# A three-stage latent transformer kernel: the first latent group's opening dealt out anew over the engines, four key products side by side, and identity products on TensorE while it waits

## The chip, the cores and the metric

The kernel runs on one core of one Trainium2 chip. The metric is device time in microseconds (us), the median over several executions. The engines are named as in the profile: PE (TensorE matmul), PEld (its weight load), DVE (VectorE), ACT (ScalarE), POOL (GpSimd) and SP (SyncE, which issues most of the DMAs).

## The reference, cut to what matters

`x` has shape (16, 64, 512), the context (16, 512, 512). Three residual blocks follow one another; the change is in the first steps of the first block.

```python
x = x + _L0_xattn_ref(ctx_1024, _layernorm(x), mask, g_x, b_x, g_l, b_l, w_q, w_kv, w_out, g_o, b_o)
x = x + _L0_attn_ref(_layernorm(x), Wq, Wk, Wv, Wo, ...)
x = x + _L0_ffn_ref(_layernorm(x), w_gate, w_up, w_down)

def _L0_xattn_ref(x, latents, mask, g_x, b_x, g_l, b_l, w_q, w_kv, w_out, g_o, b_o):
    xn = _ln(x, g_x, b_x)                        # the context
    ln = _ln(latents, g_l, b_l)                  # the 64 latents of each batch
    q = ln @ w_q
    kv_in = jnp.concatenate([xn, ln], axis=1)
    k, v = jnp.split(kv_in @ w_kv, 2, axis=-1)
    ...                                          # 8 heads of 64, softmax over 512 + 64 keys
    return _ln(out @ w_out, g_o, b_o)
```

## The kernel before, in words

The 16 x 64 latent rows are eight tiles `x0` to `x7` of 128 rows by 512. `_latents` makes q, k and v of the latents (products named `lq`, `lk`, `lv`), two tiles at a time: four groups of two tiles. Then `cross_attention` runs over the 16 batches, and after it come self-attention and the feed-forward block. All weights and activations of the large products are split into a high part (rounded to fp32r) and a low part (the remainder), so that a product is three terms: high x high, low x high, high x low, each over four chunks `k` of 128 of the contraction (`Common.terms`, the matmuls of L121).

A group of latents is made by these helpers of `_latents`:

- `moments(p)` (L494 to L500): bn_stats and bn_aggr of tile `p` on DVE, then two one-column instructions on POOL that make the reciprocal root.
- `norm(p)`: one DVE instruction over 128x512 into `lz`.
- `turn(p)` (L506): four PE transposes of `lz` into PSUM `lt` (L171), then four instructions of 128x128 that apply gain and offset into `ln`, on ACT (L520), or on DVE for tile 1 (L518).
- `upper(p)` and `lower(p)`: DVE makes the high part `lnh` (L526) and the low part `lnl` (L532).
- `high(name, w, k)` (L479): ACT rounds chunk `k` of a weight into its high part. `low(name, w, k)` (L483): DVE or POOL subtracts it for the low part. The raw weights `raw_k`, `raw_q`, `raw_v` (four chunks of 256 KB each) come by DMA into nine buffers, so that the last three chunks of `raw_v` wait for a chunk of `raw_k` to be done with.
- `bias("q", k)` (L538, L541): DVE adds up the raw query weight's chunks, weighted by `b_x`, into `ws_bq`; `bias_sum` sums that over the partitions on PE (`bq`, L549) and takes it out on DVE (L556).
- `CrossWeights.load` and `turn`: four small DMAs of the vectors g_l, b_l, b_x, g_x into `vec_rows`, one PE transpose (`vec_t`), one ACT copy (`vec`), and b_l - b_x on POOL.

`heads(g, what, ...)` makes the products `lk` or `lq` of group `g`: four column blocks of 128, each of 12 matmuls with 256 columns, taken out by ACT into `kst` (L600) or `qst` (L602). For the keys of group 0 `late = 3`: the first three blocks run together, term by term, and the fourth after them. `values(g)` makes `lv`, 24 matmuls with 512 columns. PSUM has three buffers for `mm`/`tr` tiles, two for `two` (tag "sim"), one for `av`.

The order of instructions on each engine is the order of the program text, with work that is spread over the products in between: `during(n, f)` puts `f` behind the n-th column block (`then()` is called after each). The opening, ahead of the first product, is written out at the end of `_latents`: loads, `moments(0)`, `cw.turn()`, `norm(0)`, and so on. Engines take their instructions in order; an instruction that waits holds up those behind it on its engine.

Of the kernel before, what the change touches and what calls it, by code (L numbers as in the profile page):

```python
# [9 lines left out]
F32 = mybir.dt.float32  # L10
# [4 lines left out]
ALU = mybir.AluOpType  # L15
# [4 lines left out]
P = 128  # L20
D = 512
KC = D // P
# [11 lines left out]
LN_EPS = 1e-5  # L34
# [11 lines left out]
def f32(t):  # L46

    return t.bitcast(F32)


class Common:
# [62 lines left out]
    def terms(self, ps, parts, ks, start=True, stop=True):  # L114

        terms = [(0, 2), (0, 3), (1, 2)]
        n, last = 0, len(terms) * len(ks) - 1
        for i, j in terms:
            for k in ks:
                p = parts(k)  # L120
                self.nc.tensor.matmul(  # L121
                    ps, lhsT=p[i], rhs=p[j], start=start and n == 0, stop=stop and n == last
                )
                n += 1
            yield

    def split(self, hi, lo, src, by=None):

# [86 lines left out]
GT = GB // 2  # L215
# [80 lines left out]
class Context:  # L296
# [74 lines left out]
class CrossWeights:  # L371
# [13 lines left out]
    def load(self, pool):  # L385
        self.rows = pool.tile([len(self.NAMES) * KC, P], F32, tag="vec", name="vec_rows")
        for n, name in enumerate(self.NAMES):
            self.cm.nc.sync.dma_start(
                self.rows[n * KC : (n + 1) * KC, :], self.i[name].rearrange("(c p) -> c p", p=P)
            )  # L390

    def turn(self):
        cm, nc = self.cm, self.cm.nc
        n = len(self.NAMES) * KC
        pt = cm.tr("vec_t")[:, :n]
        nc.tensor.transpose(pt, self.rows, cm.ident[:n, :n])
        nc.scalar.copy(self.vec, pt)

        nc.gpsimd.tensor_tensor(self.bl, self.bl, self.bx, ALU.subtract)


class SelfConstants:
# [52 lines left out]
def _latents(ctx, tc, cm, sc, i, cw, cx, sa):  # L455
    nc = tc.nc
# [12 lines left out]
    def load(*tiles):  # L469
        for p in tiles:  # L470
            nc.sync.dma_start(cm.x[p], i["x"][p * P : (p + 1) * P, :])
# [3 lines left out]
            raws[name, k] = pool.tile([P, D], F32, tag="raw", bufs=9, name=f"raw_{name}_{k}")  # L475
            nc.sync.dma_start(raws[name, k], source[name][k * P : (k + 1) * P, :])

    def high(name, w, k):
        nc.scalar.copy(w[0][:, k, :], raws[name, k])  # L479

    def low(name, w, k, by=None):
        by = by or (nc.vector, nc.gpsimd)[k % 2]
        by.tensor_tensor(w[1][:, k, :], raws[name, k], f32(w[0][:, k, :]), ALU.subtract)  # L483
# [6 lines left out]

    def moments(p):
        st = cm.small.tile([P, 6], F32, tag="st", name=f"st_l_{p}")  # L494
        mv = mvs[p] = cm.small.tile([P, 2], F32, tag="mv", name=f"mv_l_{p}")
        nc.vector.bn_stats(st, cm.x[p])
        nc.vector.bn_aggr(mv, st)
        r = mv[:, 1:2]
        nc.gpsimd.tensor_scalar(r, r, 1.0 + LN_EPS, LN_EPS * LN_EPS, ALU.mult, ALU.add)
        nc.gpsimd.tensor_tensor(r, r, cm.mhalf[:, :1], ALU.pow)  # L500
# [5 lines left out]
    def turn(p):  # L506
# [7 lines left out]
        ln = pool.tile([P, KC, P], F32, tag="ln", bufs=2, name=f"ln_{p}")  # L514
        for k in range(KC):
            src, scale, bias = pt[:, k * P : (k + 1) * P], cw.gl[:, k : k + 1], cw.bl[:, k : k + 1]
            if p == 1:
                nc.vector.tensor_scalar(ln[:, k, :], src, scale, bias, ALU.mult, ALU.add)  # L518
            else:
                nc.scalar.activation(ln[:, k, :], src, AF.Identity, bias=bias, scale=scale)  # L520
        rows[p] = ln

    def upper(*tiles):
        for p in tiles:
            g, n = divmod(p, GT)
            nc.vector.tensor_copy(lns[g][0][:, :, n * P : (n + 1) * P], rows[p])  # L526

    def lower(*tiles):
        for p in tiles:
            g, n = divmod(p, GT)  # L530
            hi, lo = (t[:, :, n * P : (n + 1) * P] for t in lns[g])
            nc.vector.tensor_tensor(lo, rows.pop(p), f32(hi), ALU.subtract)  # L532

    def bias(name, k):

# [45 lines left out]
    def during(n, do, *args):  # L581

        todo.setdefault(n, []).append((do, args))
# [9 lines left out]
    def heads(g, what, w, dst, scale, bias=None):  # L593

        hi, lo = lns[g]
        st = pool.tile([P, KC, GT * P], F32, tag=f"{what}st", name=f"{what}st_{g}")

        def take(m, ps):
            if bias is None:
                nc.scalar.copy(st[:, m, :], ps)  # L600
            else:
                nc.scalar.activation(  # L602
                    st[:, m, :], ps, AF.Identity, bias=bias[:, m : m + 1], scale=scale
                )


        late = 3 if (g, what) == (0, "k") else 0
        lag = 2 if (g, what) == (0, "q") else 0
        made, ready = [], []
        for m in range(KC):  # L610
            cols = slice(m * P, (m + 1) * P)
            ps = cm.mm(f"l{what}_{g}_{m}")[:, : GT * P]
            terms = cm.terms(
                ps,
                lambda k, cols=cols: (w[0][:, k, cols], w[1][:, k, cols], hi[:, k, :], lo[:, k, :]),
                range(KC),
            )
# [12 lines left out]
        for at, done, _ in ready:  # L630
            take(at, done)
        nc.sync.dma_start(dst[g], st)

    def values(g):
        hi, lo = lns[g]
        for n, p in enumerate(groups[g]):
# [1068 lines left out]
```

## Time and profile before

| | us |
|---|---|
| median of 5 runs | 918.62 (918.1 to 919.25) |
| the profiled execution's own time | 918.1 |
| its span, first to last instruction | 916.3 |
| PE busy in the span | 896.1 |
| DVE / ACT / POOL busy | 688.8 / 392.8 / 328.9 |
| first matmul of `lk` (group 0) | 11.67 |
| first matmul of `lv` (group 0) | 28.25 |

Times in the profile count from the start of the span. 1.8 us of the profiled execution's time lie outside the span. The columns of the stage rows are: stretch, its length, then busy time and number of instructions for PE, PEld, DVE, ACT and POOL, the granted clock, the DMA engines' share and GB/s. A timeline row gives start, length, engine, line, operation, out<-in, shape, count, and in brackets the idle time before and what ended it.

### The profile page before, as it was taken

To read this page: it belongs to the slowest core of one execution; us is meant where nothing else is said; L and a number is where in the kernel's file an instruction comes from. 1 tells how busy PE (TensorE), PEld (TensorE's weight loads), DVE (VectorE), ACT (ScalarE), POOL (GpSimd) and SP (SyncE) were. 2 spreads that over 40 slices of the span, in tenths; PEclk is the share of its full clock that TensorE was granted. 3 is DMA by queue.
4 is the path that set the end of the run, shared out by engine and by line. 5 is a ranking of instruction groups with operands and counts; after the bars stand their busy time and mean duration, and the time that the engine had idled before them with its cause. 6 is when DMAs were issued, how large, how long until landed. Compare 5 with 4: busy or idle time off the path is not lost.

```text
span 916.3 us, 17531 instructions
## 1 busy us (share of the span) xinstructions
PE 896.1 (98%) x6774; PEld 741.0 (81%) x6774; DVE 688.8 (75%) x1386; ACT 392.8 (43%) x750; POOL 328.9 (36%) x376
## 2 busy tenths in 40 slices
PE   5999999999999999999999999999999999999998
PEld 5898777878787788787878887878778788888886
DVE  7544477788799787786987864576887698888875
ACT  4464444444454444444544455434444333322221
POOL 5245153335253353252533522565564320100000
PEclk9999999999999999999999999999999999999999
DMA  7564565554564445444644351140005530000000
GB/s 237 177 242 138 161 185 158 170 162 143 150 187 153 140 146 165 129 132 139 201 134 147 105 169 70 48 184 3 1 1 232 206 138 12 13 12 12 13 12 23
DMA packets 80234, 111.11 MB, mean 121 GB/s; under 512 B 33160, under 2 KB 38808, under 8 KB 78872
## 3 DMA queue, kind: packets, MB, share of 16 engines
q1 hardware_dynamic: 79992, 109.48, 36.6%
q8 instruction: 53, 0.87, 0.4%
q0 software_dynamic: 160, 0.52, 0.2%
q14 instruction: 29, 0.24, 0.1%
HBM read 84.26 MB, written 25.72 MB: 120 GB/s over the span
## 4 chain that ended last, share of the span: by engine, by line
PE 88%; DVE 7%; ACT 2%; issue 1%; POOL 1%; DMA 0%; DVEq 0%; ACTq 0%; POOLq 0%
PE pv L121 19%; PE pk L121 19%; PE gu L121 13%; PE dn L121 7%; PE av L904 4%; PE sim L836 4%; PE prt L171 3%; PE lv L121 2%; PE po L121 2%; PE lq L121 2%; PE lk L121 2%; PE wo L121 2%; PE Wv L121 2%; PE ht L171 1%; PE Wq L121 1%; PE Wk L121 1%
## 5 line engine op out<-in xcount | busy, mean ns | idle before, releaser
L121 PE MATMUL pv<-xvh,x 128*128 128x512 f32 x512 | 133.1, 392 | 0.0
L121 PE MATMUL pk<-x,xkh 128*128 128x512 f32 x512 | 130.5, 397 | 0.0
L121 PEld LDWEIGHTS pk<-x,xkh 128*128 128x128 f32 x512 | 93.7, 188 | 25.5 <-issue 3.9
L121 PEld LDWEIGHTS pv<-xvh,x 128*128 128x128 f32 x512 | 95.3, 188 | 23.3 <-issue 2.2
L810 DVE TENSOR_TENSOR k<-pk,row 128x512 f32<-128x512 f32 x64 | 43.7, 684 | 46.3 <-PE pk L121 46.2
L823 ACT ACTIVATE v<-pv,rs 128x512 f32<-128x512 f32 x64 | 43.9, 686 | 79.3 <-PE pv L121 79.2
L859 ACT ACTIVATE pr<-pr,least 128x576 f32<-128x576 f32 x64 | 49.2, 772 | 55.4 <-DVE least L855 55.1
L368 POOL TENSOR_TENSOR x<-raw,x 128x512 fp32r<-128x512 f32 x32 | 43.7, 1365 | 78.0 <-ACT x L362 71.8
L121 PE MATMUL pk<-x,xkl 128*128 128x512 f32 x256 | 68.7, 390 | 0.0
L121 PE MATMUL pv<-xvl,x 128*128 128x512 f32 x256 | 68.5, 389 | 0.0
L121 PE MATMUL gu<-uT,fx 128*128 128x512 f32 (+1 forms) x288 | 67.3, 377 | 0.0
L121 PE MATMUL gu<-gT,fx 128*128 128x512 f32 (+1 forms) x288 | 65.5, 375 | 1.1 <-DVE h L1541 0.6
L121 PEld LDWEIGHTS gu<-gT,fx 128*128 128x128 f32 x288 | 52.2, 188 | 9.0 <-ACT fx L129 0.9
L121 PEld LDWEIGHTS gu<-uT,fx 128*128 128x128 f32 x288 | 51.9, 188 | 7.2
L121 PEld LDWEIGHTS pk<-x,xkl 128*128 128x128 f32 x256 | 48.1, 188 | 10.4
L121 PEld LDWEIGHTS pv<-xvl,x 128*128 128x128 f32 x256 | 48.1, 188 | 10.2
L855 DVE CUSTOM_DVE_ANT_0 pr<-sim,mask 128x576 f32<-128x576 f32 x64 | 45.9, 755 | 6.3 <-PE sim L836 5.6
L121 PE MATMUL dn<-dT,hh 128*128 128x512 f32 x176 | 44.8, 394 | 0.6 <-ACT hh L129 0.6
L321 DVE BATCH_NORM_STATS2 cst<-nat 128x6 f32<-128x512 f32 x64 | 42.8, 669 | 3.4 <-DMA nat<-in_ctx_dram 3.4
L205 ACT ACTIVATE qe_h<-qe_h,mmagic 128x512 f32<-128x512 f32 (+1 forms) x24 | 16.5, 688 | 67.2 <-DVE qe_h L202 64.1
L871 ACT COPY prT<-prt 128x512 f32<-128x512 f32 x64 | 34.1, 585 | 18.1 <-PE prt L171 18.1
L904 PEld LDWEIGHTS av<-v,prT 128*64 128x64 f32 x1024 | 36.7, 138 | 5.6 <-issue 5.6
(302 smaller groups left out, 1976.5 us busy)
## 6 DMA issues: line engine op xcount, KB each, us to landing
nat<-in_ctx_dram SPq DMA_DIRECT2D x16, 1024.0 KB
raw<-in_ctxT_dram SPq DMA_DIRECT2D x64, 256.0 KB
d_d<-qhl_d SPq DMA_DIRECT2D x11, 512.0 KB
row<-rs_d SPq DMA_DIRECT2D x16, 256.0 KB
g_d<-qhl_g SPq DMA_DIRECT2D x8, 512.0 KB
u_d<-qhl_u SPq DMA_DIRECT2D x8, 512.0 KB
gT<-g_d SPq DMA_DIRECT2D x4, 1024.0 KB
uT<-u_d SPq DMA_DIRECT2D x4, 1024.0 KB
```

The lines of the kernel that those rows point to most:

```text
L121: self.nc.tensor.matmul(ps, lhsT=p[i], rhs=p[j], start=start and n == 0, stop=stop and n == last)
L171: self.nc.tensor.transpose(pt[:, c * P : (c + 1) * P], src[:, c * P : (c + 1) * P], self.ident)
L205: nc.scalar.activation(e, e, AF.Relu, bias=self.mmagic, scale=MAGIC)
L321: nc.vector.bn_stats(st, self.nat[b][:, j, :])
L368: by.tensor_tensor(lo, self.raw[:, c, :], f32(hi), ALU.subtract)
L810: nc.vector.tensor_tensor(k[:, S : S + N], ps, cx.row[b], ALU.mult)
L823: nc.scalar.mul(v, ps, cx.rs[b][:, t : t + 1])
L836: nc.tensor.matmul(pss[r][c * S : (c + 1) * S, h, :half], lhsT=queries[b % 2][rows, m, :], rhs=st["k"][m][rows, at : at + half], start=Tru ...
L855: nc.vector.tensor_tensor_reduce(two(pr), ps[:, :, :half], two(mask), -1.0, BIG, ALU.add, ALU.min, least)
L859: nc.scalar.activation(pr, pr, AF.Exp, bias=least, scale=-1.0, accum_out=st["tot"][:, t : t + 1])
L871: nc.scalar.copy(prT, pt.rearrange("p (j q) -> p j q", q=P))
L904: nc.tensor.matmul(st["av"][rows, 2 * a + r, :], lhsT=w[:, rows], rhs=v[:, at : at + S], start=(n == 0), stop=(n == len(pairs) - 1),)
```

## The change

The change is in the opening and in the order of some work behind it:

- The four `vec_rows` DMAs are issued by ACT, ahead of its table load, in place of SP.
- For tiles 0 and 1 the first of the two one-column instructions runs on DVE; `stats(1)` runs before `norm(0)`. b_l - b_x moves behind both roots on POOL.
- Key weights: chunks 0 and 1 are rounded on ACT ahead of `turn(0)`, chunk 2 on DVE ahead of `norm(1)`, chunk 3 on ACT behind tile 1's share.
- Tile 1's gain and offset: chunks 0 and 1 on ACT, 2 and 3 on DVE (all four on DVE before). `upper(0)` comes before, `upper(1)` behind it.
- `late = KC`: all four key blocks of group 0 run side by side, one matmul of each in turn, since `terms` now yields after each matmul; the fourth block lies in the `av` buffer of PSUM. All other products keep their order.
- All four low parts of the query weight are made on DVE (two of them on POOL before).
- Value weights: the high parts of chunks 0 to 3 are called behind blocks 3 to 6 and the low parts behind 4, 4, 7, 7 (1 to 4 and 2 to 5 before).
- `busy(n)`: n matmuls of the 128x128 identity with itself into a PSUM tile `idle` that nothing reads: 4 before `vec_t`, 6 behind it, 2 behind the transposes of tile 0, 4 behind those of tile 1.

In the built program the engines' orders differ from before in this opening alone, but for one ACT instruction far behind: `fz` of tile 2 (L166, at 700.06 us) stands two instructions later.

```diff
@@ Common.terms
                 n += 1
-            yield
+                yield
@@ CrossWeights
-            self.cm.nc.sync.dma_start(
+            self.cm.nc.scalar.dma_start(
...
-        nc.gpsimd.tensor_tensor(self.bl, self.bl, self.bx, ALU.subtract)
+    def less(self):
+
+        self.cm.nc.gpsimd.tensor_tensor(self.bl, self.bl, self.bx, ALU.subtract)
@@ _latents
-    def high(name, w, k):
-        nc.scalar.copy(w[0][:, k, :], raws[name, k])
+    def high(name, w, k, vector=False):
+        copy = nc.vector.tensor_copy if vector else nc.scalar.copy
+        copy(w[0][:, k, :], raws[name, k])
...
+    def stats(p):
+        mvs[p, "st"] = cm.small.tile([P, 6], F32, tag="st", name=f"st_l_{p}")
+        nc.vector.bn_stats(mvs[p, "st"], cm.x[p])
...
-        nc.gpsimd.tensor_scalar(r, r, 1.0 + LN_EPS, LN_EPS * LN_EPS, ALU.mult, ALU.add)
+        by = nc.vector if p < GT else nc.gpsimd
+        by.tensor_scalar(r, r, 1.0 + LN_EPS, LN_EPS * LN_EPS, ALU.mult, ALU.add)
...
-        late = 3 if (g, what) == (0, "k") else 0
+        late = KC if (g, what) == (0, "k") else 0
...
-            ps = cm.mm(f"l{what}_{g}_{m}")[:, : GT * P]
+            name = f"l{what}_{g}_{m}"
+            ps = cm.ps_av.tile([P, D], F32, tag="av", name=name) if m == late - 1 else cm.mm(name)
+            ps = ps[:, : GT * P]
...
-            for _ in range(3):
-                for _, _, steps in made:
-                    next(steps)
+            for _ in range(3 if late else 1):
+                for _ in range(KC if late else 3 * KC):
+                    for _, _, steps in made:
+                        next(steps)
...
+    idle = cm.two("idle")[:, 0, :P]
+
+    def busy(n):
+
+        for _ in range(n):
+            nc.tensor.matmul(idle, lhsT=cm.ident, rhs=cm.ident, start=True, stop=True)
+
+    cw.load(pool)
     load(0, 1)
-    cw.load(pool)
...
+    busy(4)
+    cw.turn()
+    stats(0)
     moments(0)
-    cw.turn()
+    stats(1)
     norm(0)
     moments(1)
+    cw.less()
+    high("k", w_k, 0)
+    high("k", w_k, 1)
+    busy(6)
+    turn(0)
+    high("k", w_k, 2, True)
     norm(1)
-    high("k", w_k, 0)
-    turn(0)
-    turn(1)
-    for k in range(1, KC):
-        high("k", w_k, k)
-    upper(0, 1)
+    busy(2)
+    turn(1, range(2))
+    busy(4)
+    upper(0)
+    weighed(1, range(2, KC), True)
+    upper(1)
+    high("k", w_k, 3)
     lower(0, 1)
...
     for k in range(KC):
-        low("q", w_q, k)
+        low("q", w_q, k, nc.vector)
...
-        during(1 + k, high, "v", w_v, k)
-        during(2 + k, low, "v", w_v, k)
+        during(3 + k, high, "v", w_v, k)
+        during((4, 4, 7, 7)[k], low, "v", w_v, k)
```

More of the change, by code (lines that the diff above doesn't have):

```diff
@@ L488, in split @@
             low(name, w, k)
+    def stats(p):
+        mvs[p, "st"] = cm.small.tile([P, 6], F32, tag="st", name=f"st_l_{p}")
+        nc.vector.bn_stats(mvs[p, "st"], cm.x[p])
     def moments(p):
-        st = cm.small.tile([P, 6], F32, tag="st", name=f"st_l_{p}")
+        if (p, "st") not in mvs:
+            stats(p)
         mv = mvs[p] = cm.small.tile([P, 2], F32, tag="mv", name=f"mv_l_{p}")
-        nc.vector.bn_stats(st, cm.x[p])
-        nc.vector.bn_aggr(mv, st)
+        nc.vector.bn_aggr(mv, mvs.pop((p, "st")))
         r = mv[:, 1:2]
-        nc.gpsimd.tensor_scalar(r, r, 1.0 + LN_EPS, LN_EPS * LN_EPS, ALU.mult, ALU.add)
+        by = nc.vector if p < GT else nc.gpsimd
+        by.tensor_scalar(r, r, 1.0 + LN_EPS, LN_EPS * LN_EPS, ALU.mult, ALU.add)
         nc.gpsimd.tensor_tensor(r, r, cm.mhalf[:, :1], ALU.pow)
@@ L504, in norm, with turn @@
         cm.normalize(zs[p], cm.x[p], f"l_{p}", mvs.pop(p))
-    def turn(p):
+    def turn(p, ks=range(KC)):
         g, n = divmod(p, GT)
@@ L513, in turn, with weighed @@
         cm.transpose_chunks(pt, zs.pop(p), KC)
-        ln = pool.tile([P, KC, P], F32, tag="ln", bufs=2, name=f"ln_{p}")
-        for k in range(KC):
+        rows[p] = pt, pool.tile([P, KC, P], F32, tag="ln", bufs=2, name=f"ln_{p}")
+        weighed(p, ks)
+    def weighed(p, ks, vector=False):
+        pt, ln = rows[p]
+        for k in ks:
             src, scale, bias = pt[:, k * P : (k + 1) * P], cw.gl[:, k : k + 1], cw.bl[:, k : k + 1]
-            if p == 1:
+            if vector:
                 nc.vector.tensor_scalar(ln[:, k, :], src, scale, bias, ALU.mult, ALU.add)
@@ L520, in turn @@
                 nc.scalar.activation(ln[:, k, :], src, AF.Identity, bias=bias, scale=scale)
-        rows[p] = ln
     def upper(*tiles):
@@ L525, in upper @@
             g, n = divmod(p, GT)
-            nc.vector.tensor_copy(lns[g][0][:, :, n * P : (n + 1) * P], rows[p])
+            nc.vector.tensor_copy(lns[g][0][:, :, n * P : (n + 1) * P], rows[p][1])
     def lower(*tiles):
@@ L531, in lower @@
             hi, lo = (t[:, :, n * P : (n + 1) * P] for t in lns[g])
-            nc.vector.tensor_tensor(lo, rows.pop(p), f32(hi), ALU.subtract)
+            nc.vector.tensor_tensor(lo, rows.pop(p)[1], f32(hi), ALU.subtract)
     def bias(name, k):
```

## The prediction

> **What bounds the kernel now.** I read the stages first: busy time in stretches of 10 us.
>
> ```profile
> core 0: us, PE busy (x) PEld busy (x) DVE busy (x) ACT busy (x) POOL busy (x), PEclk, DMA share, GB/s
> 0.00:10.00 10.00, 2.48 (x9) 1.61 (x9) 3.26 (x8) 4.91 (x10) 2.70 (x16) 1.00 0.70 220
> 10.00:20.00 10.00, 8.33 (x55) 8.36 (x56) 9.93 (x16) 6.01 (x13) 8.51 (x3) 1.00 0.86 287
> 20.00:30.00 10.00, 9.06 (x68) 8.19 (x67) 8.30 (x14) 4.70 (x13) 3.44 (x6) 1.00 0.66 228
> 30.00:40.00 10.00, 10.00 (x71) 9.33 (x70) 5.73 (x13) 2.53 (x6) 1.48 (x4) 1.00 0.49 159
> ```
>
> PE is busy 896.1 of 916.3 us. From 30 us on it is full; half of its 20 us of idle time lies ahead of that, where DVE is full (9.93 of 10 us). In the chain of waits the opening is DVE and POOL work up to `lv`, and behind that it is PE matmuls alone until past 80 us. So what the change is worth is read at one place: the first `lv` matmul, at 28.25 us. Whatever that moves, the end moves, since the waits of PE behind it (6 us in sum, none over 1.1 us) are for engines that PE itself feeds.
>
> Then the timeline up to there, the rows that decide:
>
> ```profile
> 7.67 0.55 DVE L155 TENSOR_SCALAR lz<-x,mv_l 128x512 f32<-128x512 f32 x1 [0.95 <-POOL mv_l L500]
> 8.27 1.11 PE L171 MATMUL lt<-ident,lz 128*128 128x128 f32 x4 [1.20 <-DVE lz L155]
> 9.49 1.36 DVE L518 TENSOR_SCALAR ln<-lt,vec 128x128 f32<-128x128 f32 x4 [1.28 <-PE lt L171]
> ...
> 11.49 7.44 POOL L483 TENSOR_TENSOR wql<-raw_q,wqh 128x512 fp32r<-128x512 f32 x2 [3.86 <-ACT wqh L479]
> ...
> 11.67 2.90 PE L121 MATMUL lk<-lnh,wkh 128*128 128x256 f32 x12 [2.29 <-DVE lnh L526]
> 12.65 2.49 DVE L483 TENSOR_TENSOR wkl<-raw_k,wkh 128x512 fp32r<-128x512 f32 x4
> ...
> 16.26 1.52 DVE L538 TENSOR_SCALAR ws_bq<-raw_q,vec 128x512 f32<-128x512 f32 x1
> ...
> 17.81 4.16 DVE L541 SCALAR_TENSOR_TENSOR ws_bq<-raw_q,vec,ws_bq 128x512 f32<-128x512 f32 x3
> ...
> 22.14 0.95 PE L549 MATMUL bq<-ones,ws_bq 128*128 128x1 f32 x8
> ...
> 24.95 1.51 DVE L155 TENSOR_SCALAR lz<-x,mv_l 128x512 f32<-128x512 f32 x1
> ...
> 28.25 1.18 PE L121 MATMUL lv<-wvh,lnh 128*128 128x512 f32 x4
> ```
>
> Three landmarks: `lk` starts at 11.67, `bq` at 22.14 (as soon as DVE has `ws_bq`, 21.97), `lv` at 28.25. The same DVE forms have two lengths: `ws_bq` L538 1.52 us here, 0.48 us at 27.64 (`ws_bv`); `lz` 1.51 and 0.55 us. The long ones lie beside a POOL tensor_tensor, and POOL's own `wql` took 6.0 and 1.48 us. The two engines hold each other up.
>
> **The change, step by step.** *To the first `lk`.* The landings in the trace's DMA records: x0 3.46, x1 4.10, the vectors 4.15 to 4.70, raw_k 5.63, 7.20, 8.24 and 9.42. With the vectors off SP its raw_k issues start 1.37 us earlier (they began at 3.02, behind four issues from 1.65). The queue stood nearly idle from 3.6 to 4.1, so about 0.7 us of that arrives: I put raw_k chunk 2 at 7.5. Bounds: 8.24 as now, and 6.8, when the bytes of x, the vectors and three chunks had gone by at the GB/s of the stages. This matters because of a new wait: DVE rounds chunk 2 ahead of `norm(1)`, and takes its work in order. Behind that wait stand `norm(1)`, both `upper` and all low parts; for `norm(1)` wait the transposes of tile 1 and every `lk`. So `norm(1)` starts at 7.55 + 0.43 (an `lnh` cast of that size) = 8.0, against 7.67 now: 0.3 us lost; at bounds 7.3 (its root is ready at about 6.8) and 8.7. The root's DVE instruction, 0.13 (the small `bq` row) for POOL's 0.19 and a handover of 0.08, gains 0.1, under this wait.
>
> Then 0.55 `lz`; 1.11 transposes; two instructions of 128x128 on ACT and DVE each in place of four on DVE (1.36 / 2 = 0.7); `upper(1)` 0.43 alone, `upper(0)` being done before. 8.0 + 0.6 + 1.15 + 0.75 + 0.4 = 10.9, less about 0.1 if the transposes are partly quicker: **`lk` at 10.8**, 0.9 earlier. ACT has rounded chunk 3 by about 11, before the twelve matmuls ahead of it are through.
>
> *TensorE's rate.* Single matmuls of `lk` start 0.213 us apart from 11.68 to 15.66, and 0.120 apart from 15.80 on, for the same 256 columns, though the profile's granted clock says 1.00 throughout; the trace's clock record begins at 15.70. So 18 slow matmuls cost 18 x 0.093 = 1.7 us. The 16 identity products are meant for that. Each is like a transpose (0.213 apart), so 3.4 us in four bursts between about 1.4 and 10.2; all lie in waits, and the last four (0.85) fit under the 1.2 us from the transposes to `upper(1)`. If that cover were gone, it would cost those 0.85 us. What they bring the trace does not show: eight transposes in two bursts did not lift the rate. Bounds: nothing (1.7 us stay) and all of it. I take the middle, 0.85 us left, since the bursts make PE work on and off from 6 us instead of from 11.7, with gaps of over 1 us left.
>
> The Trainium skill speaks against this part: "TensorE: Matmul & The Clock Gate", Part 1, has the clock freed by a busy window of about 3.4 us, free-running, not by a number of matmuls. The change in rate 4.0 us after `lk` began agrees; by that rule scattered bursts bring little, and the sum below would be some 0.5 us worse.
>
> *`lk` to `bq`.* PE: 48 matmuls x 0.120 = 5.76, plus 0.85 slow, from 10.8: 17.4. Side by side all four blocks end together, so `lq` waits for the first `kst` copy (0.44, of which some 0.1 is covered): 17.75. 24 matmuls of `lq`: 20.6. DVE: `lower` 1.2 and four `wkl` 2.4 from 10.8 to 14.4; four `wql` 2.4 (two more than now, 1.2): 16.85; `ws_bq` 0.48 + 3 x 0.75 (the three of `ws_bv`) = 2.75: 19.6, where it takes 5.7 now beside POOL. POOL's next large work, `wvl` chunk 1, needs ACT's `wvh`, which now stands behind four `kst` copies and is ready at about 19.7, so the overlap is gone; if it were all there, `ws_bq` would end at 22.5. So PE, not DVE, comes last, and **`bq` starts at 20.6**, 1.5 earlier.
>
> *`bq` to `lv`.* `bq` 0.8, `lq` blocks 2 and 3 2 x 1.45 (DVE reaches the `bq` copy by 21.5, so block 3 finds its buffer), transposes 2 x 0.5: 25.3. Now this takes 6.1, because `lz` of tile 2 took 1.51 beside POOL and the root of tile 3 stood behind `wvl` on POOL until 26.17. After the change that `wvl` stands behind both roots, and `wvl` chunk 1 in front of them: 19.75 + 1.75 = 21.5, then roots by 22.4 and 23.8, `lz` of tile 3 by 24.4, or 25.3 if it is stretched. I take **`lv` at 25.6**, so 2.6 to 2.7 us gained. Value chunk 2's low part, on DVE behind `ws_bv`, ends at about 26.2 and is wanted at 27.
>
> Edits at no cost: ACT's four issues (0.3 each) push its table load of 1.28 to about 3.3, ahead of `vec` at 4 or so; `less` is wanted at 7.1 and runs by 7; the `av` buffer is free long before `bq`; `fz` of tile 2, two places later at 700 us, moves about 0.7 us of ACT work that nothing waits for there (bounds: 0.3 either way).
>
> The sum against the profiled execution: 918.1 - 2.6 = 915.5. The median of the runs is 918.62, 0.5 above it, so the forecast for the median is 916.0.
>
> **The rivals.** (a) *The transfers rule the opening.* raw_k chunk 2 lands at 8.24 as now, since its packets straggle (7.20, 8.24, 9.42 come 1.0 to 1.6 apart, against 0.65 to 0.7 for raw_q), and the rate stays low throughout. For it: ACT's `wqh` copies from 10.12 on, 0.66 apart, follow the landings. Then `lk` starts at 11.5, `lq` block 1 ends at 22.2, `lv` starts at 27.2: gain 1.1, 917.5.
>
> (b) *POOL takes over the critical place, and it gets slower.* `wvl` chunk 1 stands ahead of the roots of tiles 2 and 3 on POOL. If it takes 6.0 us, as `wql` did beside eight back-to-back DVE tensor_tensors, it runs from 19.75 to 25.8, the roots end at 26.6 and 27.4, `lz` of tile 3 at 28 or, stretched, at 29; `lv` starts at 29.6 to 30: 1.5 us slower, 920.1. It decides from an end of `wvl` at about 24.4 on. Against it: only one such DVE instruction (`wvl` chunk 0, 0.69) is left beside it.
>
> (c) *The identity products free the clock before `lk`.* Then the transposes take 0.63 (as at 27.87), `lk` starts at 10.3 and needs 5.8, `lq` block 1 ends at 19.3, and DVE's `ws_bq` (19.2) is level with it: `bq` at 19.4, `lv` at about 24.8, held by POOL's roots: gain 3.5, 915.1.
>
> **How the numbers follow.** Main case 0.48, (c) 0.22, (a) 0.23, (b) 0.07. A change of 0.2%, 1.84 us, is about what a measurement of this kernel can tell from none, so faster means under 916.8. The main case with its bounds (chunk 2 by 0.7, rate by 0.85, `lz` by 0.9) gives 914.9 to 917.1 and is faster nearly always (0.45); (c) always (0.22); (a) in a few (0.03). Same: the rest of (a) and of the main case, and some of (b): 0.24. Slower: 0.06. The range takes in (c) and (a) with half a microsecond about them: 914.6 to 917.8.
>
> **What would show it.** Right: `lk` first at 10.5 to 11.2, its four blocks interleaved; `ws_bq` L552 three times at 0.75; a bracket on DVE's `wkh` naming raw_k; `bq` released at 20 to 21; `wvl` on POOL under 2.5 us; `lv` near 25.6, and PE full behind it. Wrong: `norm(1)` later than 8.7, a `wvl` of over 4 us ahead of the roots, an `lk` as slow as now through its first 18 matmuls, or new idle time of PE behind 30 us that gives the gain back.

## The result, and the profile after

The changed kernel takes 919.1 us (median of 38 runs, 917.64 to 921.7) where the kernel before takes 917.88 (74 runs, 916.93 to 919.25): ratio 1.0015, 95% interval 1.0011 to 1.0019. So it is slower by 0.15%, a step inside the 0.2% that the prediction called about what a measurement can tell; with this many runs the sign is clear. Forecast were 916.0 and a range of 914.6 to 917.8. Timed twice more, beside the experiments, it came out at 1.0015 (1.0006 to 1.0023) and 1.0028 (1.0019 to 1.0037). Its profiled execution took 918.7 us, its span is 916.8; before they were 918.1 and 916.3.

The stages first, with the columns of the rows shown of before (stretch, length, PE, PEld, DVE, ACT, POOL, clock, DMA share, GB/s):

```profile
0.00:10.00 10.00, 6.89 (x35) 6.40 (x36) 3.30 (x9) 4.07 (x8) 2.28 (x14) 1.00 0.75 250
10.00:20.00 10.00, 8.50 (x69) 8.14 (x69) 9.38 (x17) 6.00 (x15) 0.26 (x1) 1.00 0.71 233
20.00:30.00 10.00, 9.11 (x65) 8.26 (x64) 8.68 (x16) 5.40 (x14) 4.09 (x6) 1.00 0.71 253
```

PE is busy 6.9 us of the first ten in place of 2.5, but what is added are the identity products; POOL has next to nothing in the second ten (0.26 for 8.51). Then the timeline of the changed kernel, the rows that answer to the landmarks:

```profile
5.00 2.93 PE L668 MATMUL idle<-ident 128*128 128x128 f32 x12
5.27 0.55 DVE L155 TENSOR_SCALAR lz<-x,mv_l 128x512 f32<-128x512 f32 x1
6.93 0.62 ACT L482 CAST wkh<-raw_k 128x512 fp32r<-128x512 f32 x1 [1.65 <-DMA raw_k<-in_w_kv_dram]
7.72 0.80 PE L171 MATMUL lt<-ident,lz 128*128 128x128 f32 x4
8.40 0.43 DVE L482 CAST wkh<-raw_k 128x512 fp32r<-128x512 f32 x1 [2.30 <-DMA raw_k<-in_w_kv_dram]
8.63 2.21 ACT L532 ACTIVATE ln<-lt,vec 128x128 f32<-128x128 f32 x6 [0.26 <-PE lt L171]
8.74 0.54 DVE L155 TENSOR_SCALAR lz<-x,mv_l 128x512 f32<-128x512 f32 x1
10.94 0.73 DVE L530 TENSOR_SCALAR ln<-lt,vec 128x128 f32<-128x128 f32 x2 [0.34 <-ACT ln L532]
12.28 2.15 PE L121 MATMUL lk<-lnh,wkh 128*128 128x256 f32 x16 [1.39 <-DVE lnh L537]
18.37 0.53 PEld L121 LDWEIGHTS lq<-lnh,wqh 128*128 128x128 f32 x4 [0.31 <-ACT kst L611]
18.58 3.24 DVE L552 SCALAR_TENSOR_TENSOR ws_bq<-raw_q,vec,ws_bq 128x512 f32<-128x512 f32 x3
21.97 1.02 PE L560 MATMUL bq<-ones,ws_bq 128*128 128x1 f32 x8 [0.47 <-DVE ws_bq L552]
25.19 1.50 DVE L155 TENSOR_SCALAR lz<-x,mv_l 128x512 f32<-128x512 f32 x1 [0.45 <-POOL mv_l L508]
27.22 1.17 PE L121 MATMUL lv<-wvh,lnh 128*128 128x512 f32 x4
```

In the kernel before, the first transposes follow tile 0's `lz` at once:

```profile
5.95 1.12 PE L171 MATMUL lt<-ident,lz 128*128 128x128 f32 x4 [0.87 <-DVE lz L155]
```

`lk` starts 0.6 us later than before (12.28 for 11.67), `bq` 0.2 earlier, `lv` 1.03 earlier (27.22 for 28.25). So the opening gained 1 us, not 2.6. And the end did not come 1 us earlier: from the start of the first `lv` to the start of the program's last matmul it is 885.32 us, where it was 883.81. **More was lost behind `lv` than won ahead of it**, in a stretch where the two programs' engines have the same work in the same order. That loss is the first thing to find.

Its places come out when each matmul is compared with the one before at its distance from `lv`. It comes in steps: 0.81 us in the first group of `sim` products (96.7 us), 0.67 at the `av` products of 246 us, just ahead of the eleventh such group (each of the 16 batches has two); the rest is scattered. The kernel before at both places:

```profile
97.73 1.20 PE L836 MATMUL sim<-k,mask 64*64 64x288 f32 x16
...
99.03 1.45 SPq L799 DMA_DIRECT2D k<-k_d  x1
...
241.63 1.10 DVE L368 TENSOR_TENSOR x<-raw,x 128x512 fp32r<-128x512 f32 x1
...
242.66 0.68 DVE L290 TENSOR_TENSOR qhl_g<-qhl_g 128x512 fp32r<-128x512 f32 x1
...
245.77 0.34 PE L904 MATMUL av<-vl,prl 128*64 128x64 f32 x4
```

And the changed kernel. SPq rows are SP's issues of DMAs, with the time that the issue took:

```profile
93.56 1.69 SPq L829 DMA_DIRECT2D k<-k_d  x1
...
96.68 2.03 PE L867 MATMUL sim<-k,mask 64*64 64x288 f32 x16
...
230.08 1.49 SPq L830 DMA_DIRECT2D k<-k_d  x1
...
239.40 0.71 DVE L287 STREAM_TRANSPOSE qhl_g<-qw_g 128x512 f32<-128x512 f32 x1 [0.81 <-DMA g_d<-qhl_g]
...
241.23 0.68 DVE L368 TENSOR_TENSOR x<-raw,x 128x512 fp32r<-128x512 f32 x1
...
241.41 1.66 POOL L368 TENSOR_TENSOR x<-raw,x 128x512 fp32r<-128x512 f32 x1 [2.16 <-ACT x L362]
...
241.83 1.78 DVE L290 TENSOR_TENSOR qhl_g<-qhl_g 128x512 fp32r<-128x512 f32 x1
...
246.06 0.34 PE L935 MATMUL av<-vl,prl 128*64 128x64 f32 x4 [0.67 <-ACT prl L920]
```

An issue of a small key load normally takes 0.59 us. In each kernel a few take 1.1 to 1.7. Before, one of these is at 99.03, behind the first `sim`, and harms nothing. After, one is at 93.56, ahead of it: the loads behind it in SP's queue come a microsecond later, and the `sim` that reads the last of them takes 2.03 in place of 1.20. At 230 us the held issue stands in SP's queue ahead of a store (`g_d`), which goes out 0.9 us late against PE's work; DVE's transpose waits 0.81 us for it, and ACT's and POOL's steps behind that come as much later. So POOL's `x` lies otherwise over the two DVE rows of 241 us: they take 0.68 and 1.78 us in place of 1.10 and 0.68, 0.68 more in sum, and PE then waits 0.67 for what ACT makes of them.

What holds the issue? The trace's DMA records have a queue that moves nothing but packets of 16,384 bytes, one at a time, each 0.9 to 1.9 us on one DMA engine. The page's table of queues (packets, MB, share), before and then after:

```profile
q8 instruction: 53, 0.87, 0.4%
```

```profile
q8 instruction: 54, 0.88, 0.4%
```

PE executes 6,774 matmuls and as many weight loads before: 868,352 bytes in 53 packets are about 64 bytes for each of them, so that a packet would hold 256. And from one packet's start to the next PE starts 252 of them on average before, 253 after. So the queue is read here as PE's code. One such packet starts at 98.78 us before, 0.25 ahead of the long issue; after, at 93.77 and 229.98, within 0.25 of the two long issues. The identity products are the reason that they moved: 16 products are 64 instructions of code (an fp32 product is two weight loads and two matmuls, the x12 of the row above for six products), 4 KB, so every later packet holds other work and comes earlier against it. The packet that comes 70.5 us behind `lv` before comes 66.5 behind it after.

The Trainium skill, "Runtime: NRT & Kernel Launch", section "Instruction fetch mechanics", states that an engine's code is streamed in blocks of 16 KiB over a queue of its own, mostly hidden. The packets agree. These rows suggest besides that SP's issues are not spared; how firm that is, the experiments have to say.

### The profile page after: what moved, and what is told of

Its sections match the earlier page's. It is cut to its first block, busy times and chain, and to the rows that moved or that the text cites. A ratio compares the mean times of both kernels' runs of the same rounds, so it can differ in the third digit from the quotient of the medians.

```text
span 916.8 us, 17590 instructions
## 1 busy us (share of the span) xinstructions
PE 900.8 (98%) x6806; PEld 745.1 (81%) x6806; DVE 688.7 (75%) x1389; ACT 392.8 (43%) x751; POOL 321.4 (35%) x372
## 4 chain that ended last, share of the span: by engine, by line
PE 88%; DVE 7%; ACT 3%; issue 1%; DMA 1%; POOL 1%; ACTq 0%; SPq 0%; DVEq 0%; POOLq 0%
PE pv L121 19%; PE pk L121 18%; PE gu L121 13%; PE dn L121 7%; PE av L935 4%; PE sim L867 4%; PE prt L171 3%; PE lv L121 2%; PE po L121 2%; PE lq L121 2%; PE lk L121 2%; PE wo L121 2%; PE Wv L121 2%; PE ht L171 1%; PE Wq L121 1%
```

## The experiments

Landmarks of the profiled executions, in us; "to the end" is the distance from the start of the first `lv` to the start of the last matmul. The ratio is to the kernel before on the same chip; the runs r and e, f and g, h, and j were timed on four different chips, so across these groups only ratios compare.

| run | `lk` | `lv` | to the end | median | ratio, 95% interval |
|---|---|---|---|---|---|
| before | 11.67 | 28.25 | 883.81 | 917.88 | 1 |
| after | 12.28 | 27.22 | 885.32 | 919.1 | 1.0015 (1.0011 to 1.0019) |
| r0_after | 12.42 | 27.37 | 886.00 | 919.01 | 1.0015 (1.0006 to 1.0023) |
| e1_no_identity | 13.03 | 28.51 | 884.07 | 918.67 | 1.0009 (1.0 to 1.0017) |
| e2_k2_on_act | 12.96 | 27.91 | 885.11 | 919.35 | 1.0015 (1.0006 to 1.0024) |
| e3_vec_on_sp | 12.66 | 27.60 | 884.28 | 918.47 | 1.0008 (0.9999 to 1.0017) |
| f0_before_ends_first | 11.66 | 28.24 | 883.41 | 917.98 | 1.0001 (0.9992 to 1.001) |
| f1_after_ends_first | 13.05 | 27.99 | 885.41 | 919.09 | 1.0013 (1.0005 to 1.0022) |
| g0_new_opening | 11.13 | 26.08 | 885.04 | 917.09 | 0.9989 (0.998 to 0.9998) |
| g1_new_ends_first | 11.50 | 26.45 | 884.66 | 916.84 | 0.9986 (0.9977 to 0.9995) |
| h1_before_16_tiny | 11.57 | 28.13 | 885.26 | 919.63 | 1.0013 (1.0004 to 1.0022) |
| h2_before_10_tiny | 11.70 | 28.26 | 884.07 | 918.76 | 1.0005 (0.9996 to 1.0014) |
| h3_after_wide | 12.63 | 27.58 | 884.13 | 918.94 | 1.0009 (1.0001 to 1.0018) |
| h4_new_wide | 10.91 | 25.85 | 884.90 | 916.75 | 0.9984 (0.9976 to 0.9993) |
| j1_wide_timed | 12.59 | 27.53 | 885.27 | 918.11 | 1.0002 (0.9994 to 1.0011) |
| j2_after_timed | 12.24 | 27.18 | 885.83 | 919.99 | 1.0028 (1.0019 to 1.0037) |

### The parts of the opening

Four kernels: the changed one again, and with one part undone each.

`r0_after`, the changed kernel once more.

> The changed kernel once more, beside the kernel before on the same chip, for a second profile of its opening. If the loss comes from the opening itself, lv starts at 27 to 28.5 us again and the span follows it; the first profile had lt of tile 0 at 7.72 (behind identity products until 7.93), raw_k chunk 2 rounded on DVE at 8.40 and lk at 12.28. If the transfers' straggling rules, these three move by over 0.5 us between the two profiles, and lk with them. Time: 1.0 to 1.4 us above the kernel before.

`e1_no_identity`: no identity products, and no PSUM tile for them (the lines that make the tile and `busy` are left out here).

```diff
-    busy(4)
     cw.turn()
...
-    busy(6)
     turn(0)
...
-    busy(2)
     turn(1, range(2))
-    busy(4)
     upper(0)
```

> The changed kernel without any of its 16 identity products; all else as changed. Theory 1 (the identity products stand in the way: each is two PE instructions, and twelve of them run from 5.00 to 7.93, so that the transposes of tile 0 wait 1.8 us): lt starts at 5.9, lk at 11.7 or earlier, but at the slow rate for 4 us, which gives 1.7 us back; the time falls by 0.3 to 1 us against the changed kernel. Rival 2 (DVE's wait for raw_k chunk 2 rules the path anyway): lk starts at 11.9 to 12.3 as changed and is slow on top: 1.5 to 2 us slower than the changed kernel.

`e2_k2_on_act`: DVE does not wait for key chunk 2 ahead of `norm(1)`.

```diff
     turn(0)
-    high("k", w_k, 2, True)
     norm(1)
...
     upper(1)
+    high("k", w_k, 2)
     high("k", w_k, 3)
```

> The changed kernel with chunk 2 of the key weight rounded on ACT, behind tile 1's share and ahead of chunk 3, so that nothing stands before norm(1) on DVE. Theory 2 (the wait for raw_k on DVE is what delays tile 1): lz of tile 1 at 6.8 in place of 8.74, and lk up to 1 us earlier; time 0.5 to 1 us lower than changed, and less spread between runs. Rival 1 (identity products and transposes of tile 0 end later than that anyway): lt of tile 1 only moves to about 8.9, since PE is held by lt of tile 0 until 8.4, and the gain is under 0.4 us.

`e3_vec_on_sp`: the vectors go back to SP, between `x` and the key chunks.

```diff
-            self.cm.nc.scalar.dma_start(
+            self.cm.nc.sync.dma_start(
...
-    cw.load(pool)
     load(0, 1)
+    cw.load(pool)
```

> The changed kernel with the four vector loads issued by SP between x and raw_k, as before. If issuing them from ACT pays (raw_k earlier), this is 0.5 to 0.7 us slower than the changed kernel. If the raw_k transfers straggle whenever they start and the vectors land at 4.7 either way (4.68 in the changed kernel, 4.70 before), it is the same within 0.3 us; if the vectors' packets on a second queue disturb x and raw_k, it is faster by 0.3 to 1 us and raw_k chunk 0 lands at about 5.6 in place of 6.9.

What follows from them:

- *The identity products* do both. Without them the first transposes are back at 6.11 us (7.72 in the changed kernel) and 13 of the first 48 `lk` matmuls are slow (1 with them; 18 before); `lv` is at 28.51, 1.3 later than with them. And the distance to the end is 884.07, 1.25 shorter than with them. What they win ahead of `lv` they lose behind it: the last matmul of the two profiles is at 912.54 and 912.58. By its median e1 is 0.34 us under r0, which is no difference that shows (918.15 to 919.99 against 918.16 to 920.75); `lk` at 13.03 is far from the 11.7 that theory 1 had.
- *The wait for key chunk 2* is real: without it `lz` of tile 1 is at 6.87 in place of 8.74. But `lk` does not come earlier (12.96), since the transposes of tile 1 wait behind identity products, and since the halves of the gain and offset still follow each other, as in the changed kernel. The wait was one of three things in a row, and the time that theory 2 had (0.5 to 1 us less) did not come: 919.35 for 919.01.
- *The vectors on ACT* bring key chunk 2 at most a little: DVE starts on it at 8.69 with them on SP, at 8.40 and 8.14 in two profiles with them on ACT. And chunk 0 comes later by them: ACT starts on it, as it lands, at 5.59 with the vectors on SP (5.64 before), at 6.93 and 6.71 with them on ACT, though it is issued 1.4 us earlier.
- *Behind `lv`* e3 loses 0.70 us at the first `sim`, where a held issue of 1.40 us stands at 65.92 behind `lv`, and nothing at 246 us, though PE's code is that of the changed kernel and only the vectors' issues differ. So the place of PE's code alone does not fix the price.

### Where the loss behind lv is, and a better opening

The loss at the first `sim` looked like a load that comes with no slack, so two kernels issue two steps of the first batch ahead of its keys; and two have a new opening.

`f0_before_ends_first` on the kernel before, `f1_after_ends_first` on the changed one:

```diff
+    around(0, 0, 1)
     begin(0)
     mask(0)
-    around(0, 0, 1, 2, 3)
+    around(0, 2, 3)
     around(1, 0, 1)
```

> The kernel before with one reorder behind the opening: at the start of cross-attention SP issues the four small loads of latent keys that the first sim reads (k<-k_d) ahead of the mask, query and value loads of batch 0 instead of behind them. Theory P (the first sim meets the landing of these loads with no time to spare, so that an issue held up on SP is paid there): before's own profile shows sim at 1.20 us without a wait, so here nothing or up to 0.3 us is gained. Rival R (the loss behind lv is spread over chance stalls of single transfers, wherever they hit): the same time as before within 0.3 us, with the same spread of runs.

> The changed kernel with the same reorder. Theory P: the first sim takes 1.2 us in place of 2.0 to 2.4, the distance from the first lv to the second pk returns to 70.6 us (71.4 and 71.8 in two profiles of the changed kernel), and the time falls by 0.7 to 1 us against the changed kernel. Rival R: the stall is replaced by others and the time falls by under 0.3 us.

`g0_new_opening`: vectors on SP; 4 identity products ahead of the vectors' transpose, 2 behind it, 4 behind the transposes of tile 1; no wait for a key chunk ahead of `norm(1)`; tile 0's gain and offset ahead of the key chunks on ACT; tile 1's all on DVE. The lines that put the vectors back on SP are those of e3. `g1_new_ends_first` has the order of f1 besides.

```diff
-    high("k", w_k, 0)
-    high("k", w_k, 1)
-    busy(6)
+    busy(2)
     turn(0)
-    high("k", w_k, 2, True)
     norm(1)
-    busy(2)
-    turn(1, range(2))
+    turn(1, ())
     busy(4)
-    upper(0)
-    weighed(1, range(2, KC), True)
-    upper(1)
+    high("k", w_k, 0)
+    high("k", w_k, 1)
+    high("k", w_k, 2, True)
+    weighed(1, range(KC), True)
+    upper(0, 1)
     high("k", w_k, 3)
```

> The changed kernel with the opening put right by the first profiles: vectors on SP again; 2 identity products behind vec_t in place of 6, none between the two tiles' transposes, 4 behind them; norm(1) ahead of the rounding of key chunk 2 on DVE; on ACT tile 0's gain and offset ahead of the key weights; tile 1's wholly on DVE. Theory 1+2 (twelve identity instructions, the wait for raw_k on DVE and ACT, and ACT's and DVE's halves of one tile one after the other delay lk): lt of tile 0 at 6.0, lz of tile 1 at 6.9, lk at 10.5 to 11.3 in place of 12.3 to 12.4, at the fast rate from about 10 to 12 us on, lv at 25.7 to 26.3. Rival (raw_k's landing at 8.1 to 8.7 rules in any order): lk not before 11.8. For the time: if all of the 1.2 us passed on, 917.7; if the first sim takes it back (theory P), 918.5.

> The opening of the run before with the small key loads first as well. Theories 1, 2 and P together: lv at 25.7 to 26.3, no wait at the first sim, 916.2 to 917.2, below both kernels. Rival R (chance stalls take any lead back): 918 or more.

The reorder changes nothing in the kernel before, and in the changed one it only puts the stall in another place: 0.78 us are lost ahead of the first `sim`, where PE waits for the load `mask<-q_d`. A held issue (1.25 us, at 90.48) stands ahead of that load too; it lies beside a packet not of PE's queue but of the trace's other instruction queue, q14 (8,192 bytes). So theory P missed, and it came as rival R had it: another stall in place of the first. The order alone is not the cause.

The new opening is faster than both kernels. `lk` and `lv` are where theories 1 and 2 had them. In its timeline the gain and offset of tile 1 begin at 8.95 on DVE, without waiting for ACT, and `lk` starts at 11.12:

```profile
8.95 1.36 DVE L530 TENSOR_SCALAR ln<-lt,vec 128x128 f32<-128x128 f32 x4
...
11.12 2.14 PE L121 MATMUL lk<-lnh,wkh 128*128 128x256 f32 x16 [1.32 <-DVE lnh L537]
```

`lv` at 26.08 is 2.2 us earlier than before, but 1.2 of it is given back on the way to the end: 0.66 between 119 and 125 us, and 0.67 ahead of the eleventh group of `sim`, as in the changed kernel. Neither the reorder nor the new opening takes all of this loss away.

### PE's code in its place

`h1_before_16_tiny`: the kernel before, with 16 products of one column, done while PE waits for the vectors. `h2_before_10_tiny` has 10.

```diff
     moments(0)
+    idle = cm.two("idle")[:1, 0, :1]
+    for _ in range(16):
+        nc.tensor.matmul(idle, lhsT=cm.ident[:, :1], rhs=cm.ident[:, :1], start=True, stop=True)
     cw.turn()
```

> The kernel before, with 16 products of one column by one column ahead of the vectors' transpose, where PE waits anyway until 4.8 us. They do no work that is used; they put 64 instructions (16 products of two weight loads and two matmuls) into PE's stream, as the 16 identity products do, and leave the opening alone. Theory F (PE's code arrives in packets of 16 KB, 256 instructions each, and the products shift every later packet against the work; a packet that falls on a small load on which PE depends delays it): lv stays at 28.2 to 28.4, the packet that arrives 70.5 us behind lv in the kernel before arrives 65 to 67 behind it, the issue of a small key load near 93 us takes 1.4 to 2.0 instead of 0.6, the first sim comes 0.6 to 1.2 late against lv, and most likely 0.3 to 0.6 more is lost near 240 us: 918.6 to 919.3 where the kernel before has 918.0. Rival C (the loss behind lv comes from the opening's own changes, such as the order of DVE's or POOL's work, or an earlier lv that meets a traffic fixed in time): nothing moves, 918.0 within 0.3, and the first sim stays within 0.2 of its place.

> The same with 10 products of one column: 40 instructions, 2.5 KB, the shift that the new openings have. Theory F: the packet arrives 68 to 69 us behind lv, where it hits no load of the first sim (0 to 0.2 late there), and a later one 204 to 205 behind lv, where it holds the issue near 230 us and costs 0.6 at the eleventh sim, as in the new openings: 918.4 to 918.7 where the kernel before has 918.0. Rival C: 918.0 within 0.3, nothing at 240 us.

`h3_after_wide`: the changed kernel, its identity products joined four to one.

```diff
-    idle = cm.two("idle")[:, 0, :P]
+    idle = cm.two("idle")[:, 0, :].rearrange("p (a n) -> p a n", n=P)
...
-        for _ in range(n):
-            nc.tensor.matmul(idle, lhsT=cm.ident, rhs=cm.ident, start=True, stop=True)
+        while n:
+            a = min(n, KC)
+            n -= a
+            nc.tensor.matmul(
+                idle[:, :a, :],
+                lhsT=cm.ident,
+                rhs=cm.ident.unsqueeze(1).to_broadcast([P, a, P]),
+                start=True,
+                stop=True,
+            )
```

> The changed kernel, with the identity products made up to four times as wide (the identity repeated as the right side, up to 512 columns), so that PE multiplies for the same time with 5 products, 20 instructions, instead of 16 products and 64 instructions. Theory F: the opening stays (lv at 27.1 to 27.4), the packet comes 69 to 70 us behind lv, the first sim loses nothing (0 to 0.2, where the changed kernel loses 0.8 to 1.2), near 240 us at most 0.3 is lost: 917.0 to 917.8, faster than the kernel before by 0.2 to 1.0. Rival C: the loss stays and the time is the changed kernel's, 918.7 to 919.3.

`h4_new_wide` is the same edit on `g1_new_ends_first`.

> The new opening with the ends first, with the ten identity products as three wide ones of the same columns: 12 instructions instead of 40. Theory F: lv at 26.2 to 26.6, the packet comes 207 us behind lv instead of 204, the 0.64 us that the new opening loses near 240 us is gone: 916.0 to 916.5 where the new opening with the ends first had 916.84. Rival C: 916.8 within 0.3, and the loss near 240 us stays.

The timeline of h1. The products are over by 2.3 us, long before the vectors land:

```profile
1.35 0.94 PE L658 MATMUL idle<-ident 128*1 128x1 f32 x32 [1.35 <-POOL ident masks.py:199]
...
97.03 1.10 SPq L801 DMA_DIRECT2D k<-k_d  x1
97.56 0.71 PE L839 MATMUL sim<-k,mask 64*64 64x288 f32 x6
...
98.81 1.18 PE L839 MATMUL sim<-k,mask 64*64 64x288 f32 x10 [0.55 <-DMA k<-k_d]
...
247.13 0.34 PE L907 MATMUL av<-vl,prl 128*64 128x64 f32 x4 [0.68 <-ACT prl L892]
```

`lv` stands where it was (28.13), and then a key load is issued in 1.10 us instead of 0.59, the first `sim` is cut in two by a wait for that load, and at 247 us the 0.67 us wait of the changed kernel is there to a hundredth. The distance to the end is 1.45 us longer than before, as in the changed kernel (1.51), and the kernel is 0.13% slower (1.0004 to 1.0022), by its median a little above the 918.6 to 919.3 expected. In the opening the products do one thing more: 24 of the first 48 `lk` matmuls are slow, for 18, and `bq` starts at 22.60, for 22.14; `lv` does not show it. The PSUM tile that the products write could be a rival, since it takes a turn of the two `sim` buffers; but it is there with 10 products too, and nine of the eleven times with 16 lie above all eleven with 10. The packet came at 96.79, not at the 93 to 95 that was expected, but two microseconds earlier than before and just ahead of a load, which it held for 1.10 us and not for 1.4 to 2.0; the moves of the packets are not as even as the theory had them. With 10 products the first `sim` loses nothing, the wait at 246 us is there (0.67), though the issue that stands long near 232 us is not a key load but one of `raw` (0.84 us for 0.38), and 0.34 is won elsewhere; 1.0005 (0.9996 to 1.0014) is between the two and, taken alone, tells nothing.

The wide products of h3 take the same time of PE with a third of the instructions (4.89 to 7.82 us, 2.93, for 4 matmuls in place of 12), and these two losses are gone from its profile:

```profile
97.02 1.20 PE L875 MATMUL sim<-k,mask 64*64 64x288 f32 x16
...
244.95 0.34 PE L943 MATMUL av<-vl,prl 128*64 128x64 f32 x4
```

The way from `lv` to the end is 884.13; but its timed median was 918.94, where 917.0 to 917.8 was expected: a miss, taken up below. h4 is faster than both kernels of the change, 916.75 (ratio 0.9984, 0.9976 to 0.9993), but over g1 it does not show the 0.6 that was expected, and its time lies where the rival had it (916.8 within 0.3): the wait near 245 us only went from 0.67 to 0.43. There no issue ahead of the store `g_d` was held; it went out in time, and DVE's transpose still waited 0.35 us for it.

### What varies from one execution to the next

Two more profiles of h3, one of the changed kernel, one of h1; each expectation names two theories of why h3's times lay higher than its profile.

> The changed kernel with wide identity products once more, for another execution's profile. Theory O (the opening varies): lv between 27.2 and 29, most likely later than 27.6, and the distance from lv to the last matmul again 883.9 to 884.4, so the time moves with lv. Theory B (losses behind lv vary): lv 27.4 to 27.8 and the distance 884.1 to 886.5, with a new stall at a load that a packet of code holds.

> The same a third time, with the same expectations: theory O has lv move and the distance stand at 883.9 to 884.4, theory B the other way round.

> The changed kernel a third time. Theory O: lv 27.0 to 28.5, the distance from lv to the last matmul 885.3 to 886.0 as in the two profiles there are. Theory B: lv 27.1 to 27.5, the distance 884.5 to 887.

> The kernel before with 16 products of one column once more. By the theory of the code packets the places repeat: the first sim late by 0.6 to 1.3 or, where the packet just misses the loads, not at all; near 240 us 0.5 to 0.7 late again; lv 28.1 to 28.4; 918.0 to 919.8.

Then h3 and the changed kernel, timed side by side.

> The changed kernel with wide products, timed beside the changed kernel. By the theory of the code packets alone it is 1.0 to 1.5 under the changed kernel, 917.6 to 918.2, and its times lie within 0.8 of their median. If something that the profiles do not show takes the gain back, it is 918.5 to 919.2, with times up to 920 and more, and at most 0.6 under the changed kernel.

> The changed kernel beside it: 918.8 to 919.3, with times from 918 to 921, by both theories.

| run | `lv` | to the end | that execution's time |
|---|---|---|---|
| i1_wide_again | 27.32 | 884.39 | 917.77 |
| i2_wide_third | 27.45 | 884.06 | 917.57 |
| i3_after_third | 27.65 | 885.44 | 919.24 |
| i4_tiny_again | 28.06 | 886.00 | 920.05 |

Side by side the wide products bring 918.11 (916.95 to 919.0) and the changed kernel 919.99 (917.94 to 923.19): 1.9 us, for 44 instructions of PE less and no work less. The high median of h3 in its own session was not seen again; its ratio there, 1.0009 (1.0001 to 1.0018), and the one here overlap in their intervals. The times of the wide form lie within 1.16 of their median, for the 0.8 expected, and beside the kernel before it is the same (1.0002, 0.9994 to 1.0011), though its `lv` is about 0.7 earlier. The opening does not make the spread, against theory O: over eight profiles of the changed kernel and its wide form `lv` stays between 27.18 and 27.65. The distance to the end does: 884.1 to 885.3 in the four of the wide form, 885.3 to 886.0 in the four of the changed kernel. In the profile of j1 the loss is back, by a wait at another place:

```profile
121.45 2.14 PE L121 MATMUL pk<-x,xkh 128*128 128x512 f32 x8 [0.42 <-DVE k L849]
```

So the place of the code, as far as these few profiles tell, sets the odds of a stall in each execution, and not a fixed price.

How firm is the link from packet to issue? In the 20 profiles of this study there are 2,560 issues of the small key loads. 72 took over 1.1 us; beside 68 of these (94%) a packet of PE's code begins, from 0.6 us ahead of the issue to 0.4 behind it. Of the 2,488 others this holds for 84 (3%). Read the other way, 68 of the 152 issues beside such a packet are long (45%), and 4 of the 2,408 others (0.2%); each of these four has a packet of q14 starting 0.2 to 1.1 us ahead of it. The limits of 1.1, 0.6 and 0.4 us were chosen after the rows had been seen. That small instructions without work, added or joined, make and unmake the loss is shown by h1, and by j1 beside j2, in which `lv` does not move with it. That the place of the code and the held issue are the way is a coincidence of records, 68 times over, with the waits behind it seen. Why a packet on one DMA engine holds SP's issue is open.

## Why the prediction was wrong, point by point

- **"Whatever that moves, the end moves": failed, and decided the sign.** It was read from the waits of PE behind `lv`, small and on engines that PE itself feeds. The sum put the loss behind `lv` at nothing. But loads issued by SP meet the work with less than 1 us to spare (an issue held 1.1 us longer cost the first `sim` 0.81), and the change moved what these collide with. `lv` came 1.03 earlier; the distance behind it grew by 1.51 in that profile, and by 1.51 to 2.19 in the four there are. "New idle time of PE behind 30 us that gives the gain back" stood among the signs of being wrong, with no price and no rival of its own.
- **"Each is like a transpose (0.213 apart)", "all lie in waits": failed.** An identity product is two matmuls, about 0.5 us together (2.07 for the first four, 2.93 for the six), not one of 0.213. Six of them took 2.93, longer than the wait that they lay in: `lz` of tile 0 was ready at 5.82, its transposes started at 7.72 (before: 5.95).
- **raw_k chunk 2 at 7.5: failed.** It landed at 8.4, as rival (a) had it (8.24), so `norm(1)` was at 8.74 and not at 8.0. In the four profiles of the changed kernel DVE begins on it at 8.14 to 8.48. With the vectors on SP it begins at 8.69, 8.61 and 8.98 (e3, g0, g1), and in h4 the chunk is there by 7.48. So the 0.7 us that the move was to bring this chunk stand out of no scatter, and chunk 0 came 1.0 to 1.5 us later by it (6.62 to 7.06 in the four profiles, 5.59 in e3), not earlier.
- **"Two instructions of 128x128 on ACT and DVE each in place of four": failed.** They did not run side by side. DVE's two began at 10.94, when ACT's row (8.63 to 10.84) was through, and the bracket names ACT; both write the one tile `ln`. From the end of tile 1's transposes (9.99) to the end of the last of these instructions (11.67) it took 1.68 us, for 0.75 in the sum; besides the 0.34 us that DVE waits for ACT, ACT was busy with tile 0 until 10.13, and `upper(0)`, for which that had to be done, stood ahead on DVE. With all four on DVE, g0 has them done at 10.31, 1.4 earlier than here, but g0 differs in other things too, so the price of the split alone stays open.
- **0.85 us left of the slow rate: too much.** 1 of 48 `lk` matmuls was slow; the rate was free from 8.12 on by the trace's clock record. Rival (c) had the clock right and all else wrong (`lk` at 10.3). PE had then worked without a break since 5.00, 3.1 us. The Trainium skill, "TensorE: Matmul & The Clock Gate", Part 1, speaks of a busy window of about 3.4 us. The row agrees roughly, 3.1 being a little less. The identity products freed it: without them (e1) the record begins at 15.90. The long burst that delayed the transposes was not needed for that: with two products in its place g0 has the rate free from 9.20 on, still ahead of `lk`.
- **`lk` to `bq`: right in part.** The wait of `lq` for `kst`, 0.31 for 0.35, was right. `ws_bq` L552 took 3.24 for three, not 2.25, with POOL's `wvl` beside it (19.74 to 21.28), so DVE and not PE came last: `bq` waited 0.47 for it.
- **`bq` to `lv` in 5.0: right.** It took 5.25 (6.11 before); `lz` of tile 3 was the stretched one, 1.50, the bound that the prediction named. Rival (b) did not come: `wvl` took 1.54, not 6.0.
- Rival (a)'s `lv` at 27.2 was met to a hundredth, by other terms: a later `lk` than it had, and a free clock. Its 917.5 fell with the first point.

The sum in one line: 2.6 forecast, less 1.6 in the opening (`lk` 1.5 later than forecast, of which 1.4 is left at `bq`, and 0.25 from `bq` to `lv`), less 1.5 to 2.2 behind `lv`. With the opening mended (h4) `lv` is at 25.85, 0.25 from the forecast of 25.6, and the kernel 1.5 us faster than before (916.75 for 918.27 in that session). Even that gives back 1.1 of its 2.4 us; how much of this is chance and how much an earlier `lv` that shortens a store-to-load chain was not told apart.

## What to carry to other kernels

An instruction that does no work is not free because its engine idles: it moves all code behind it, and where loads arrive just in time, that can, by all that these records show, move a stall into the path hundreds of microseconds later. If an engine must be kept busy, do it with few wide instructions, not with many small ones (918.11 for 919.99 us here). And a gain at one place is a gain at the end only where the loads behind it have slack: measure the distance from the landmark to the end, in both kernels, before believing a faster opening. Two engines that each write half of one tile may take turns; give the tile to one of them, and time that first.

## What was not expected of the hardware

- PE's code comes in packets of 16,384 bytes, one for 256 instructions, each 0.9 to 1.9 us on a DMA engine, and of SP's issues of small key loads that meet one 45% take 1.1 to 2.0 us instead of 0.59 (68 of 152).
- 64 instructions of PE that take 0.94 us in a wait cost about 1.2 us (0.4 to 2.0) at the end of a 918 us kernel (h1).
- An fp32 product of 128x128 by 128 columns is two loads and two matmuls, about 0.5 us in a burst (2.93 for six); an fp32 transpose of that size is one of each.
- One product of 512 columns takes PE as long as four of 128 (2.93 us for the six in both forms).
- Where DVE and POOL hold each other up, 0.9 us more or less decide what it costs: at 241 us two DVE rows took 1.10 and 0.68 us before and 0.68 and 1.78 after, when POOL's row began 0.9 us later against PE's work.
